# The second cross-attention of a two-layer decoder: the order of its steps, the turning of its maxima, and the order of VectorE's and ScalarE's work

## The chip, the cores and the metric

The kernel runs on one core of one Trainium2 chip. The metric is the device time of one launch in microseconds (us). Before the change it was 882.6 us, the median of three runs (882.2 to 886.55). The profile comes from one further execution, which took 881.06 us.

## The reference, cut to what matters

The reference is a decoder of two layers in float32, on 8 sequences of 128 tokens with 256 features. Each layer has a self-attention, a cross-attention against a context, and a feed-forward part, and after each of them a residual is added and a layer norm taken. The feed-forward part of the second layer is a mixture of 64 experts, of which each token uses 8. The change touches the second layer's cross-attention and the routing that follows:

```
def _L1_xattn_ref(q, k, v):              # x, context, context: (8, 128, 256)
    h = 8                                # the 128 ROWS are split into 8 heads of 16
    qh = q.reshape(b * h, d // h, m)     # (64, 16, 256)
    ...
    qk = jnp.einsum('bdm,bdn->bmn', qh, kh) * scale      # 256 x 256 per head
    sm = jax.nn.softmax(qk, axis=-1)
    ret = jnp.einsum('bmn,bcn->bcm', sm, vh)
    return ret.reshape(b, c, m)
...
x = _layernorm(x + _L1_xattn_ref(x, ctx_2048, ctx_2048), axis=-1)
x = _layernorm(x + _L1_ffn_ref(x, ...), axis=-1)    # logits, softmax, top 8 of 64 experts
```

So the attention runs over the features: in each head 16 rows are contracted and a 256 x 256 matrix of scores is made.

## The kernel before, in words

The program is one straight line of stages. The part in question begins at about 467 us of the profiled execution and ends at about 613 us, when the number of tokens of each expert is known (`full`, L984). After that come the sorting of the token-expert pairs and 104 visits to experts, which need those numbers.

*Heads and units.* The 128 rows of one sequence hold eight heads of 16 rows. They are handled as four blocks of 32 rows (index j, which is also a strip of 32 rows of TensorE), each with two heads, called parity 0 and 1. A unit is a pair (b, par): sequence b, parity par. There are 16 units, worked through by `run_pipelined`: in step n, unit n is in its first stage, unit n-1 in its second, and so on, and within a step the deepest stage is issued first.

*Stages of a unit* (line numbers as in the profile):

- `limits` (L803): GpSimd makes `y_qm`, the rows of this parity alone. TensorE makes scores `y_s` in four tiles, one for each block j (L812), for one half c of the 256 query columns and for both parities, and VectorE takes the negated maximum of each into the tile `maxima` (L820). Half c is tied to par, so both units of a sequence are needed before its maxima are complete.
- `shift` (L824): TensorE turns the maxima of this parity (two transposes, `y_m`, L827). VectorE adds them to `y_qm` (L829) and gives `y_q`. The maxima lie in a row of each head that the other head leaves free; the matching row of `keys` holds ones, so that the next product subtracts the maximum by itself.
- `weights` (L832): eight products `y_sT` (L836), transposed scores less their maximum, then four exponentials `y_e` by ScalarE (L843).
- `weigh` (L848): 16 products with the values (`y_av`) and 16 with ones (`y_z`), both at L855. For parity 1 VectorE then takes the reciprocal of the sums (L862, 128 x 256), multiplies (L864), GpSimd adds the residual (L866), and `layernorm` follows: statistics and their aggregate on VectorE (L187, L189), the reciprocal root on GpSimd (L181, L182), the subtraction and scaling on VectorE (L192).
- `turn_x` (L869), only for five of the units: the normed rows of one or two sequences are written to memory, turned by TensorE (`pt_moe`, L880) and copied by ScalarE (`xT_moe`, L884).
- `choose` (L887): the experts' logits (`gate`, L894), the eight largest (L901), those eight removed (`match_replace`, L903), the mask and the running count `seen`.
- `place` (L912): each pair's position among its expert's (`pos`, L924 and L925; `slot1`, L930), then the softmax over the logits: the exponentials `r_e` on ScalarE (L944), the reciprocal (L949) and the weights `comb` (L951).

The list at L966 gives the depths: limits 0, nothing 1, shift 2, weights 3, weigh 4, nothing 5, turn_x 6, choose 7, place 8. `idle` fills the empty places. In the first three steps `finish_heads` lets TensorE end the self-attention before (`l_y`).

*What sets the order.* `tc.manual_schedule(engines={nc.tensor.engine})` fixes TensorE's order as it is written. The order on VectorE, ScalarE and GpSimd is made by the scheduler of the framework. Each engine works through its own list strictly, and semaphores hold an instruction back until what it needs is there.

*PSUM.* The tiles `y_s`, `y_m`, `y_sT`, `pt_moe`, `gate`, `pos`, `count` and `base` all come from the pool `ps_x` with six banks, handed out in rotation: a tile can be written when the one requested six places earlier has been read by all its readers. `y_av` and `y_z` have two banks of their own.

Of the kernel before, what the change touches and what calls it, by code (L numbers as in the profile page):

```python
# [52 lines left out]


def idle(st, *unit):
    pass
# [3 lines left out]
def decoder_kernel(ctx: ExitStack, tc: tile.TileContext, i, out):  # L60
# [608 lines left out]
    def make_constants():  # L669

        nc.gpsimd.memset(before, 1.0)
        nc.gpsimd.affine_select(
            before, before, pattern=[[1, P]], compare_op=ALU.is_gt, fill=0.0, base=0, channel_multiplier=-1
        )
        nc.gpsimd.iota(iota, pattern=[[1, P]], base=0, channel_multiplier=0, allow_small_or_imprecise_dtypes=True)
        nc.gpsimd.iota(starts, pattern=[[P, P]], base=0, channel_multiplier=0, allow_small_or_imprecise_dtypes=True)
        nc.gpsimd.iota(
            numbers, pattern=[[S, B]], base=0, channel_multiplier=1, allow_small_or_imprecise_dtypes=True
        )
        nc.gpsimd.tensor_scalar(numbers, numbers, 1.0 / (B * S), 1.0, ALU.mult, ALU.add)  # L680
        nc.gpsimd.iota(turns, pattern=[[1, TOP]], base=0, channel_multiplier=0, allow_small_or_imprecise_dtypes=True)
        nc.gpsimd.iota(rows_16, pattern=[[1, P], [0, TOP]], base=0, channel_multiplier=0, allow_small_or_imprecise_dtypes=True)
        nc.gpsimd.tensor_scalar(rows_16, rows_16, -MIDDLE, None, ALU.add)
        nc.gpsimd.iota(blks_16, pattern=[[1, NG], [0, TOP]], base=0, channel_multiplier=0, allow_small_or_imprecise_dtypes=True)
        nc.gpsimd.memset(seen[:, 0, :], 0.0)
        for par in range(2):
            nc.gpsimd.tensor_scalar(keys[:, :, par, :], cx, quarter[par], one_row[par], ALU.mult, ALU.add)
# [87 lines left out]
    with (  # L775
# [4 lines left out]
        tc.manual_schedule(engines={nc.tensor.engine}),  # L780
# [3 lines left out]
        for n in range(2):  # L784
            t = ap.tile([P, 2, 2, P], F32, name=f"maxima_{n}")
            nc.gpsimd.memset(t.rearrange("p a c r -> p (a c r)"), 0.0)
            maxima.append(t)
        for par in range(2):
# [10 lines left out]
            sums_w.append(t.rearrange("p two r -> p (two r)"))  # L799
        def rows_at(j):  # L800
            return slice(32 * j, 32 * j + 32)

        def limits(st, b, par):  # L803
# [12 lines left out]
            flat = maxima[b % 2].rearrange("p par c r -> p (par c r)")  # L816
            for j in range(4):

                at = c * P + 32 * j + 16
                nc.vector.tensor_reduce(  # L820
                    flat[:, at : at + 2 * P - 15 : 2 * P - 16], tiles[j], AX.X, ALU.max, negate=True
                )

        def shift(st, b, par):  # L824
            pt = ps_x(f"y_m_{b}_{par}")[:, : 2 * P]
            for c in range(2):
                nc.tensor.transpose(pt[:, c * P : (c + 1) * P], maxima[b % 2][:, par, c, :], ident)  # L827
            t = xp.tile([P, D], F32, tag=f"qs{par}", name=f"y_q_{b}_{par}")
            nc.vector.tensor_tensor(t, pt, st["q"], ALU.add)  # L829
            st["q"] = t  # L830

        def weights(st, b, par):  # L832
            tiles = [ps_x(f"y_sT_{b}_{par}_{j}").rearrange("p (k m) -> p k m", k=2) for j in range(4)]
            for k in range(2):
                for j in range(4):
                    nc.tensor.matmul(  # L836
                        tiles[j][:, k, :], keys[rows_at(j), b, par, k * P : (k + 1) * P], st["q"][rows_at(j), :],
# [7 lines left out]

        held = {}

        def weigh(st, b, par):  # L848
# [18 lines left out]
            layernorm(x5[b // 2][:, b % 2, :], r, f"l1x_{b}")  # L867

        def turn_x(st, b, par):  # L869

            st["seqs"] = {(1, 1): (0, 2), (3, 1): (2, 2), (5, 1): (4, 2), (7, 0): (6, 1), (7, 1): (7, 1)}.get((b, par))
# [15 lines left out]
        def choose(st, b, par):  # L887
# [12 lines left out]
            for bb in range(n):  # L900
                nc.vector.max(top[:, bb, :], ps[:, bb, :])  # L901

                nc.vector.match_replace(rest[:, bb, :], top[:, bb, :], ps[:, bb, :], -3e38)  # L903
# [6 lines left out]
            st["logits"], st["top"] = ps, top  # L910

        def place(st, b, par):  # L912
# [19 lines left out]
            )  # L932
            if last:
# [3 lines left out]
                )  # L937

            nm = sm.tile([P, 2], F32, tag="nm", name=f"nm_r_{b0}")[:, :n]
            nc.vector.tensor_scalar(nm, st["top"][:, :, 0], -1.0, None, ALU.mult)  # L940
            e = xp.tile([P, 2, NE], F32, tag="r_e", name=f"r_e_{b0}")[:, :n]
            sums = sm.tile([P, 2], F32, tag="sums", name=f"sums_r_{b0}")[:, :n]
            for bb in range(n):
                nc.scalar.activation(  # L944
                    e[:, bb, :], st["logits"][:, bb, :], AF.Exp, bias=nm[:, bb : bb + 1], scale=1.0,
                    accum_out=sums[:, bb : bb + 1],
                )
            inv = sm.tile([P, 2], F32, tag="inv", name=f"inv_r_{b0}")[:, :n]
            nc.vector.reciprocal(inv, sums)  # L949
            for bb in range(n):  # L950
                nc.vector.scalar_tensor_tensor(  # L951
                    comb[:, b0 + bb, :], e[:, bb, :], inv[:, bb : bb + 1], st["mask"][:, bb, :], ALU.mult, ALU.mult
                )
# [3 lines left out]
        def finish_heads(step):  # L957
# [7 lines left out]
        run_pipelined(  # L965
            [(b, par) for b in range(B) for par in range(2)],  # L966
            [limits, idle, shift, weights, weigh, idle, turn_x, choose, place],
            finish_heads,
        )
# [337 lines left out]
```

## Time and profile before

| what | us |
|---|---|
| median of three runs | 882.6 |
| the profiled execution | 881.06 |
| its span, first to last instruction | 879.1 |
| first y_sT starts | 494.21 |
| last y_z ends | 601.96 |
| sequence 7 is normed (L192 ends) | 606.86 |
| `full` ends | 613.2 |
| TensorE busy | 803.5 (91%) |
| VectorE busy | 460.3 (52%) |
| ScalarE busy | 288.7 (33%) |
| mean granted clock of TensorE | 0.954 |

The first two rows are whole times of executions; the span is 1.96 us shorter than the time of its own execution. The other times count from the start of the span. "Busy" counts an engine as working from the recorded start to the recorded end of an instruction; for TensorE the ends are modelled, and waits between the members of a merged group are part of the group's duration. PE is TensorE, PEld its loading of weights, DVE VectorE, ACT ScalarE, POOL GpSimd. In a row of the timeline, the brackets at the end give the idle time of the engine just before, and what ended it. The granted clock is 1.00 at full speed.

### The profile page before, as it was taken

What the parts mean: (1) busy time and instruction counts of PE and PEld (TensorE: products, weight loads), DVE (VectorE), ACT (ScalarE), POOL (GpSimd) and SP (SyncE); (2) the same over time, 40 slices, a digit from 0 to 9 for tenths busy, and PEclk for the clock granted to TensorE, in tenths of its full rate; (3) what the DMA queues carried; (4) which work ended last, traced back from release to release, by engine and by line L of the source; (5) the groups of instructions that cost most, each with busy time, mean ns of one, the idle gap of its engine ahead of it and who ended that gap; (6) DMA issues with size and microseconds to landing.
All of it is one profiled execution on the core that took longest, in us unless ns stands there. A gap on an engine that the chain in (4) does not pass through costs nothing. (4 is left out here: it accounts for less than half of the span.)

```text
span 879.1 us, 14286 instructions
## 1 busy us (share of the span) xinstructions
PE 803.5 (91%) x4588; PEld 539.6 (61%) x4588; DVE 460.3 (52%) x1280; ACT 288.7 (33%) x990; POOL 232.9 (26%) x321
## 2 busy tenths in 40 slices
PE   8899997999999999999999999996588888999945
PEld 5455653667455558555557655553588877988834
DVE  3699886413544442344444566755795333443335
ACT  2567742221333330233330132332232332333301
POOL 0011113215100000000015121101566655555524
PEclk9999987999999999999999998987599999999979
DMA  5500011820000000000000000000579987998665
GB/s 167 157 1 1 2 48 49 293 90 1 0 1 0 1 1 0 1 0 1 1 18 31 1 14 1 13 13 13 198 227 287 296 279 224 299 309 290 203 237 228
DMA packets 39730, 87.80 MB, mean 100 GB/s; under 512 B 6432, under 2 KB 16192, under 8 KB 38752
## 3 DMA queue, kind: packets, MB, share of 16 engines
q1 hardware_dynamic: 32352, 68.96, 24.0%
q0 software_dynamic: 6144, 16.79, 5.7%
q10 hardware_dynamic: 1152, 1.05, 0.4%
q8 instruction: 41, 0.67, 0.3%
q14 instruction: 41, 0.34, 0.1%
HBM read 76.29 MB, written 10.49 MB: 99 GB/s over the span
## 5 line engine op out<-in xcount | busy, mean ns | idle before, releaser
L224 ACT ACTIVATE l_e<-l_s,nm_l 128x128 f32<-128x128 f32 x256 | 90.4, 370 | 93.2 <-DVE nm_l L221 92.9
L1142 PE MATMUL moe_gu_few<-cols,w_few 128*128 (+1 forms) x832 | 114.0, 281 | 2.2 <-issue 0.4
L1142 PEld LDWEIGHTS moe_gu_few<-cols,w_few 128*128 128x128 f32 x832 | 102.9, 195 | 7.5 <-issue 6.6
L1172 POOL DMA_INDIRECT pair_rows<-moe_os_few,pairs x64 | 63.3, 988 | 53.3 <-DVE moe_os_few L1171 41.1
L1096 POOL DMA_INDIRECT xg_few<-x_rows,tok_i x60 | 62.8, 1047 | 29.5 <-issue 11.3
L1159 PE MATMUL moe_o_few<-moe_h_few,w_few 128*128 128x128 f32 x416 | 63.9, 276 | 0.0
L843 ACT ACTIVATE y_e<-y_sT 128x512 f32<-128x512 f32 x64 | 33.0, 603 | 83.3 <-PE y_sT L836 50.6
L740 PE MATMUL l_q<-xT_l1a,w_qkv 128*128 128x512 f32 x128 | 60.2, 593 | 0.0
L740 PE MATMUL l_k<-xT_l1a,w_qkv 128*128 128x512 f32 x128 | 60.1, 592 | 0.0
L740 PE MATMUL l_v<-xT_l1a,w_qkv 128*128 128x512 f32 x128 | 60.1, 592 | 0.0
L231 DVE TENSOR_SCALAR l_e<-l_e,inv_l 128x128 f32<-128x128 f32 x256 | 58.3, 292 | 1.4
L723 DVE TENSOR_TENSOR l_vs<-l_c,l_vs 128x512 f32<-128x512 f32 x32 | 22.1, 692 | 67.4 <-PE l_c L722 67.4
L1162 ACT COPY cols<-moe_o_few 128x256 f32 (+1 forms) x104 | 38.9, 374 | 55.2 <-PE moe_gu_few L1142 18.7
L703 PE MATMUL l_y<-w_o,l_vs 128*128 128x256 f32 x256 | 56.9, 381 | 0.0
L1150 ACT ACTIVATE moe_s_few<-moe_gu_few 128x128 f32<-128x128 f32 x104 | 28.9, 279 | 79.9 <-PE moe_gu_few L1142 39.8
L1159 PEld LDWEIGHTS moe_o_few<-moe_h_few,w_few 128*128 128x128 f32 x416 | 55.2, 193 | 0.0
L703 PEld LDWEIGHTS l_y<-w_o,l_vs 128*128 128x128 f32 x256 | 48.2, 190 | 9.8 <-issue 2.8
L224 ACT ACTIVATION_READ_ACCUMULATOR l_e<-l_s,nm_l 128x1 f32 x256 | 53.2, 208 | 0.0
L1121 DVE COPY cols<-moe_xT_few 128x256 f32<-128x256 f32 x64 | 26.5, 417 | 48.2 <-PE moe_o_few L1159 21.4
L1152 DVE TENSOR_TENSOR moe_h_few<-moe_gu_few,moe_s_few 128x128 f32<-128x128 f32 x104 | 29.7, 286 | 41.5 <-ACT moe_s_few L1150 25.6
L221 DVE TENSOR_REDUCE nm_l<-l_s 128x4 f32<-128x512 f32 x64 | 43.2, 684 | 10.0 <-PE l_s L755 8.1
L748 ACT COPY l_vs<-l_v 128x512 f32<-128x512 f32 x32 | 18.8, 586 | 78.4 <-PE l_v L740 78.4
(267 smaller groups left out, 1360.0 us busy)
## 6 DMA issues: line engine op xcount, KB each, us to landing
w_few<-in_experts SPq DMA_DIRECT2D x104, 384.0 KB
z<-pair_rows SPq DMA_DIRECT2D x7, 1024.0 KB
w_qkv<-in_w_qkv SPq DMA_DIRECT2D x8, 768.0 KB
w_o<-in_w_o SPq DMA_DIRECT2D x1, 2048.0 KB
xT<-in_xT SPq DMA_DIRECT2D x2, 512.0 KB
x<-in_x SPq DMA_DIRECT2D x4, 256.0 KB
cx<-in_ctx SPq DMA_DIRECT2D x1, 1024.0 KB
q_up<-in_up_qT SPq DMA_DIRECT2D x4, 256.0 KB
```

The lines of the kernel that those rows point to most:

```text
L221: nc.vector.tensor_reduce(nm, s, AX.X, ALU.max, negate=True)
L224: nc.scalar.activation(e[:, a, :], s[:, a, :], AF.Exp, bias=nm[:, a : a + 1], scale=1.0, accum_out=sums[:, a : a + 1],)
L231: nc.vector.tensor_scalar(e[:, a, :], e[:, a, :], inv[:, a : a + 1], None, ALU.mult)
L703: nc.tensor.matmul(py[:, :D], scaled[b // 4, m][:, b % 4 * S : (b % 4 + 1) * S], w_o[:, m, :], start=(m == 0), stop=(m == L1_HEADS - 1),)
L740: nc.tensor.matmul(ps, w_qkv[:, k, c, n, :], xT[h][:, k, :], start=(k == 0), stop=(k == 1))
L843: nc.scalar.activation(e, tiles[j], AF.Exp)
L1096: nc.gpsimd.indirect_dma_start(out=x, out_offset=None, in_=xd, in_offset=bass.IndirectOffsetOnAxis(ap=tok_i[:, g : g + 1], axis=0), bounds ...
L1142: mm = nc.tensor.matmul(ps[:, a, :], ws[v][:, at : at + P], cols[:, k, bass.ds(o + P, P)], start=(k == 0), stop=(k == 1),)
L1152: nc.vector.tensor_tensor(hid, ps[:, 1, :], s, ALU.mult)
L1159: nc.tensor.matmul(ps[:, c, :], ws[v][:, at : at + P], hs[v], start=True, stop=True)
L1162: cp = nc.scalar.copy(cols[:, :, bass.ds(o, P)], ps)
L1172: inst = nc.gpsimd.indirect_dma_start(out=zd, out_offset=bass.IndirectOffsetOnAxis(ap=pairs[:, g : g + 1], axis=0), in_=o, in_offset=None, ...
```

## The change

Four things are changed in this part of the kernel.

1. *Order on TensorE.* The stages get explicit depths, and within a step they are issued as weights, weigh, apply, place, choose, turn_x, shift, limits, norm. In steps 18 to 20 it is weights, place, apply, choose, turn_x, weigh, norm, and after that turn_x, choose, place. Sequences 0 to 5 are routed one unit later than before.
2. *Maxima.* The tile `maxima` now holds both parities side by side (16 columns each), so that one pair of transposes turns both. `shift` runs for parity 0 only and makes both `y_q`, each with one scalar_tensor_tensor that keeps one parity's maxima (`one_row[par]`). The order of the two parities in `keys` is swapped to suit.
3. *Order on VectorE and ScalarE.* Both are now under `manual_schedule`: their instructions stand in the order of the program.
4. *Norm and softmax.* `layernorm` is split into `norm` (statistics, root, and a shift made by GpSimd) and `apply` one step later: an activation of ScalarE with scale and bias, except for sequence 7, which VectorE still does. In `choose`, the exponentials of the routing softmax are issued between the eight largest and `match_replace`, and in `place` the weights `comb` come ahead of the count's copy.

```
-        tc.manual_schedule(engines={nc.tensor.engine}),
+        tc.manual_schedule(engines={nc.tensor.engine, nc.vector.engine, nc.scalar.engine}),
...
-            t = ap.tile([P, 2, 2, P], F32, name=f"maxima_{n}")
+            t = ap.tile([P, 2, P], F32, name=f"maxima_{n}")
...
-                at = c * P + 32 * j + 16
-                nc.vector.tensor_reduce(
-                    flat[:, at : at + 2 * P - 15 : 2 * P - 16], tiles[j], AX.X, ALU.max, negate=True
-                )
+                at = c * P + 32 * j
+                nc.vector.tensor_reduce(flat[:, at : at + 17 : 16], tiles[j], AX.X, ALU.max, negate=True)
 
         def shift(st, b, par):
-            pt = ps_x(f"y_m_{b}_{par}")[:, : 2 * P]
+            if par == 1:
+                return
+            pt = ps_x(f"y_m_{b}")[:, : 2 * P]
             for c in range(2):
-                nc.tensor.transpose(pt[:, c * P : (c + 1) * P], maxima[b % 2][:, par, c, :], ident)
-            t = xp.tile([P, D], F32, tag=f"qs{par}", name=f"y_q_{b}_{par}")
-            nc.vector.tensor_tensor(t, pt, st["q"], ALU.add)
-            st["q"] = t
+                nc.tensor.transpose(pt[:, c * P : (c + 1) * P], maxima[b % 2][:, c, :], ident)
+            for par, head in enumerate(states[2 * b : 2 * b + 2]):
+                t = xp.tile([P, D], F32, tag=f"qs{par}", name=f"y_q_{b}_{par}")
+                nc.vector.scalar_tensor_tensor(t, pt, one_row[par], head["q"], ALU.mult, ALU.add)
+                head["q"] = t
...
-            layernorm(x5[b // 2][:, b % 2, :], r, f"l1x_{b}")
+            st["r"] = r
+
+        def norm(st, b, par):
+            if par == 0:
+                return
+            bs = sm.tile([P, 6], F32, tag="ln_st", name=f"st_l1x_{b}")
+            nc.vector.bn_stats(bs, st["r"])
+            mv = sm.tile([P, 2], F32, tag="ln_mv", name=f"mv_l1x_{b}")
+            nc.vector.bn_aggr(mv, bs)
+            rs = sm.tile([P, 1], F32, tag="ln_rs", name=f"rs_l1x_{b}")
+            rsqrt_eps(rs, mv[:, 1:2])
+            if b < B - 1:
+                off = sm.tile([P, 1], F32, tag="ln_shift", name=f"shift_l1x_{b}")
+                nc.gpsimd.tensor_scalar(off, mv[:, 0:1], rs, -1.0, ALU.mult, ALU.mult)
+                mv = off
+            st["mv"], st["rs"] = mv, rs
+
+        def apply(st, b, par):
+            if par == 0:
+                return
+            to = x5[b // 2][:, b % 2, :]
+            if b < B - 1:
+                nc.scalar.activation(to, st["r"], AF.Identity, bias=st["mv"], scale=st["rs"])
+            else:
+                nc.vector.tensor_scalar(to, st["r"], st["mv"][:, 0:1], st["rs"], ALU.subtract, ALU.mult)
...
-            st["seqs"] = {(1, 1): (0, 2), (3, 1): (2, 2), (5, 1): (4, 2), (7, 0): (6, 1), (7, 1): (7, 1)}.get((b, par))
+            st["seqs"] = {(2, 0): (0, 2), (4, 0): (2, 2), (6, 0): (4, 2), (7, 0): (6, 1), (7, 1): (7, 1)}.get((b, par))
...
                 nc.vector.max(top[:, bb, :], ps[:, bb, :])
 
+            nm = sm.tile([P, 2], F32, tag="nm", name=f"nm_r_{b0}")[:, :n]
+            nc.vector.tensor_scalar(nm, top[:, :, 0], -1.0, None, ALU.mult)
...
+            for bb in range(n):
+                nc.scalar.activation(
+                    e[:, bb, :], ps[:, bb, :], AF.Exp, bias=nm[:, bb : bb + 1], scale=1.0,
+                    accum_out=sums[:, bb : bb + 1],
+                )
+            for bb in range(n):
+
                 nc.vector.match_replace(rest[:, bb, :], top[:, bb, :], ps[:, bb, :], -3e38)
...
-        run_pipelined(
-            [(b, par) for b in range(B) for par in range(2)],
-            [limits, idle, shift, weights, weigh, idle, turn_x, choose, place],
-            finish_heads,
-        )
+        units = [(b, par) for b in range(B) for par in range(2)]
+        states = [{} for _ in units]
+        depths = {limits: 0, shift: 2, weights: 3, weigh: 4, norm: 4, apply: 5, turn_x: 6, choose: 7, place: 8}
+        for step in range(len(units) + 8):
+            if step < 18:
+                stages = weights, weigh, apply, place, choose, turn_x, shift, limits, norm
+            elif step < 21:
+                stages = weights, place, apply, choose, turn_x, weigh, norm
+            else:
+                stages = turn_x, choose, place
+            for stage in stages:
+                n = step - depths[stage]
+                if 0 <= n < len(units):
+                    stage(states[n], *units[n])
+            finish_heads(step)
```

## The prediction

> **What bounds the kernel now.** I read the page first: TensorE is busy for 91% of the span, but the share mixes stages. Then the timeline of the second cross-attention. Its matrix work runs from 494 us (first y_sT) to 602 us (last y_z); routing ends at 613.2 us with L984 (full), and everything after it hangs on that instant, so the change is worth what it moves the instant by. TensorE in one step, with the columns start, duration, instruction, idle time before it:
>
> ```profile
> 511.51 2.20 PE L836 MATMUL y_sT<-y_q,keys 32*128 32x256 f32 x16
> 513.65 0.47 PE L827 MATMUL y_m<-ident,maxima 128*128 128x128 f32 x2
> 514.05 2.10 PE L812 MATMUL y_s<-keys,x 32*128 32x512 f32 x8
> 516.08 0.64 PE L855 MATMUL y_av<-y_e,values 128*32 128x256 f32 x8
> ...
> 537.53 1.77 PE L836 MATMUL y_sT<-y_q,keys 32*128 32x256 f32 x16
> 539.23 0.44 PE L827 MATMUL y_m<-ident,maxima 128*128 128x128 f32 x2
> 540.51 3.53 PE L812 MATMUL y_s<-keys,x 32*128 32x512 f32 x8 [0.84 <-ACT r_e L944]
> ```
>
> The same groups take 1.08 (y_sT) and 1.07 us (y_s) where nothing holds them, so 2.20 and 2.10 hide waits inside the groups. The y tiles rotate through six PSUM banks: a tile waits for whoever read the tile six requests earlier. The second to fourth y_s wait for the exponentials of the y_sT just before; the third and fourth y_sT wait for the reductions of the y_s before. VectorE, in the odd steps:
>
> ```profile
> 505.89 1.76 DVE L862 RECIPROCAL y_inv<-y_z 128x256 f32<-128x256 f32 x1 [0.76 <-PE y_z L855]
> 507.68 0.42 DVE L864 TENSOR_TENSOR y_r<-y_av,y_inv 128x256 f32<-128x256 f32 x1
> 508.95 0.43 DVE L187 BATCH_NORM_STATS2 st_l1x<-y_r 128x6 f32<-128x256 f32 x1 [0.84 <-POOL y_r L866]
> 509.41 0.18 DVE L189 BATCH_NORM_AGGREGATE mv_l1x<-st_l1x 128x2 f32<-128x6 f32 x1
> 510.60 0.41 DVE L192 TENSOR_SCALAR x<-y_r,mv_l1x,rs_l1x 128x256 f32<-128x256 f32 x1 [1.01 <-POOL rs_l1x L182]
> ```
>
> VectorE waits twice on GpSimd (0.84 and 1.01) with the reductions queued behind. Last, the stretches view (busy us of PE, PEld, DVE, ACT, POOL, then granted clock):
>
> ```profile
> 505.75:517.94 12.19, 12.19 (x120) 6.39 (x116) 8.84 (x15) 4.13 (x8) 3.39 (x5) 1.00 0.01 1
> 530.73:561.29 30.56, 29.72 (x252) 15.92 (x248) 20.28 (x44) 9.43 (x21) 5.85 (x9) 0.89 0.03 10
> ...
> 538.00:541.40 3.40, 2.56 (x21) 1.47 (x16) 3.16 (x16) 1.64 (x7) 0.00 (x0) 1.00 0.01 2
> 541.40:544.80 3.40, 3.40 (x11) 1.81 (x8) 2.70 (x5) 1.01 (x3) 0.92 (x1) 0.50 0.00 0
> 544.80:548.20 3.40, 3.40 (x34) 1.49 (x33) 0.37 (x2) 0.00 (x0) 0.00 (x0) 0.50 0.00 0
> 568.70:572.10 3.40, 2.56 (x20) 1.53 (x17) 3.13 (x15) 1.78 (x7) 0.00 (x0) 1.00 0.00 0
> ```
>
> Two plain steps take 12.19 us; four steps with a routing group take 30.56. Inside each routing group the clock falls to 0.50 for 6.8 us, both times after 3.4 us in which TensorE was busy for only 2.56. In 541.4 to 548.2 the y_av/y_z group took 3.4 us, not 1.84, and y_s 3.53, not 2.53: one fall costs about 2.6 us.
>
> **The change, part by part.** In each step TensorE now runs y_sT, y_av/y_z, (routing), y_m, y_s instead of y_av/y_z, y_sT, y_m, y_s. The weighting now lies between y_sT and y_s, where it hides the exponentials, and no longer between y_s and the next y_sT, where it hid the reductions. VectorE, in program order: reciprocal and multiply (odd steps), routing, y_q, four reductions, statistics.
>
> *Odd step, laid out from the end of the weighting.* Reciprocal 1.76 and multiply 0.42 stand ahead of the reductions: 2.2. The y_s (1.07) are done by then. The fourth y_sT needs the second reduction, 0.60 + 0.68 later: 3.5. Weight load after the wait and its two halves: about 0.95, so the weighting starts at 4.45 and ends at 6.3 (1.84).
> *Even step.* One pair of turns 0.37, y_s 1.07 + 0.1 to VectorE, 1.28 for two reductions, 0.95, then 1.84: 5.75. The two y_q are now SCALAR_TENSOR_TENSOR from PSUM: between 0.42 (L829) and 0.48 (L1231), taken at 0.47 as L569, which also reads PSUM (0.463). They run during the y_s, so either bound costs nothing; without that cover it would be 0.1 a pair. Pair: 12.05 against 12.19. Gains on one side (half of the 32 turns, 8 x 0.37 = 3.0; the two waits for GpSimd; the exponentials) are spent on the exposed reductions.
>
> *Routing group, full clock.* turn_x adds four turns, 0.6. choose stands ahead of the reductions, and in the changed program match_replace waits for ScalarE's two exponentials (both read the gate bank): two MAX8 0.45, nm 0.16, exponentials 2 x (0.31 + 0.19) = 1.0, replaces 0.6, mask 0.23, seen 0.45, together 2.9. place (0.75 pos on TensorE, then slot 0.28, inv 0.15, two combine 0.5 ahead of y_q) delays the reductions by about 1.05. Sum 4.55 over four plain steps, so 28.65 where before took 30.56 and 29.46, each with a fall.
>
> *First and last steps.* The weighting of the first head pair starts 4.6 after the first y_sT (1.08 + 1.17 + 1.28 + 0.95, nothing to weigh yet), at 498.8, against 498.18. From there to the weighting of (7, 0): 7 pairs x 12.05 = 84.35, two routing groups 9.1, less 5.4 because the last two intervals have no y_s: 586.9. Before: about 593.0, so 6.1 earlier, of which 5.2 are the two falls.
>
> *Tail.* On ScalarE the last apply by activation (sequence 6) stands ahead of the copy of xT_moe for sequences 4 and 5. It needs reciprocal, multiply, add, statistics and GpSimd's root and shift (1.76 + 0.42 + 0.73 + 0.61 + 0.22 + 0.57 + 0.22, with the hops 5.0), counted from 1.7 before the weighting of (7, 0): 3.3. Then 0.60 for the activation (L1243, the same form; 0.37 as a copy is the lower bound) and 0.59 for the copy: 4.5. Queued behind that copy on TensorE are gate and the last weighting, which before ran without a break: gate to 5.6, weighting to 7.45. VectorE's choose for 4 and 5 (2.9) delays the last reciprocal to 8.5. Then 3.2 for VectorE, 1.0 for GpSimd, 0.41: sequence 7 is normed 13.15 after 586.9, at 600.05 (before 606.87). From there before took 6.33. Now gate 6 follows the turns of 7, choose 6 stands ahead of choose 7, and each has its exponential in the line to the mask: about 1.8 more. End 608.2 against 613.2: minus 5.0, if the clock never falls between 494 and 600.
>
> *The clock.* In an odd step TensorE works about 1.8 of the 3.4 us after the weighting (y_s, two y_sT, then waiting), less than the 2.56 that twice preceded a fall. A 3.4 us slice that begins within about 1.8 us there is this empty: chance about one half in each of the four plain odd steps with reductions, so 2. In the two choose steps the wait is 2.9 longer: 0.9 each. Together about 4 falls at 2.6: plus 10.4. Bounds: 0 (nothing falls) and 6 (every odd step), plus 15.6.
>
> [...] The slice at 538.0 was three quarters busy and the clock fell all the same, so the sum goes by the row.
>
> Sum against the profiled execution: 881.06 (span 879.1) - 5.0 + 10.4 = 886.5. The median, 882.6, is 1.5 above it: 888.0. Change: +5.4, where 0.5% (4.4 us) is about what can be told from no change.
>
> **The rivals.**
> *The clock holds (other side).* Place: the odd steps. With at most one fall the time is 877.6 to 880.2; it decides below two falls (5.0 / 2.6). For it: the work per pair is the same as before, and plain steps show clock 1.00 now. Against: before spread its waits over each step, this gathers them after the weighting.
> *As many falls as now.* Two, in the choose steps alone: 882.6 - 5.0 + 5.2 = 882.8.
> *VectorE streams.* If the layout is too strict and TensorE never waits on a reduction, a pair costs VectorE's own sum: 8 x 0.62 + 2.2 + 0.95 + 0.61, and gaps, about 9. Seven pairs save 20: some 868. Against: the third y_sT waits by bank, whatever VectorE's total.
> *More falls, longer tail.* Six: 893.2, and the tail's half clock may begin earlier, another 2.
> *The edit moves nothing.* A pair comes out equal anyway; this falls in with the second rival.
>
> **How the numbers follow.** Three to five falls: 0.54, centre 888.0 (885.4 to 890.6). Two falls: 0.15. None or one: 0.15. VectorE streams: 0.05. Six or more: 0.11. The range leaves out 0.05 of streaming and a little at both ends: 877 to 896. Faster by over 0.5% (below 878.2): streaming 0.05 and most of the no-fall cases, 0.13 together. Within: the rest of those, two falls, and most of three: 0.32. Slower (above 887.0): 0.55.
>
> **What would show it.** Pairs of plain steps near 12 us; in odd steps y_sT groups of 3 us or more with TensorE waiting for maxima; match_replace after r_e; a gap of about 2.5 us on TensorE ahead of gate for 4 and 5; VectorE no longer waiting 1.0 for rs_l1x but once; four stretches of clock 0.5 between 494 and 600. Wrong if that count is below two, if reductions run during the reciprocal's step without delay, or if the tail takes no longer than now.

## The result and the profile after

The changed kernel takes 889.12 us (median of 14 runs, 884.51 to 894.63), the kernel before, on the same chip, 882.42 (14 runs, 878.15 to 886.55). The medians differ by 6.7 us (0.8%); the ratio on record is 1.010, with a 95% interval of 1.0078 to 1.0123. So it is slower, by about 1%.

The profiled execution of the changed kernel took 890.04 us. Its head, its sums and two rows of 40 equal slices, from the page (sums: engine, busy us, share, instructions; the rows: PE is TensorE's busy share in tenths, PEclk its granted clock in tenths):

```profile
span 888.3 us, 14266 instructions
PE 797.9 (90%) x4572; PEld 537.9 (61%) x4572; DVE 458.2 (52%) x1273; ACT 293.1 (33%) x997; POOL 233.4 (26%) x328
PE   8899988999999999999999998986598888998855
PEclk9999996999999999999999979887599999999979
```

The same two rows of the kernel before:

```profile
PE   8899997999999999999999999996588888999945
PEclk9999987999999999999999998987599999999979
```

TensorE is busy for less (797.9 us against 803.5), and the kernel is slower all the same. The slices from the 23rd to the 28th, in which the part in question lies, show why sums over the span say little here: TensorE is less busy there (9, 9, 8, 9, 8, 6 against 9, 9, 9, 9, 9, 6), and its clock is lower on the whole (9, 7, 9, 8, 8, 7 against 9, 9, 8, 9, 8, 7).

From here on "the stage" is the stretch from the start of the first y_sT to the end of `full`. It took 118.99 us before and takes 126.83 now, 7.84 more. The rest of the 9 us between the two profiled executions lies behind `full` (265.9 against 267.4 us), where nothing was changed.

A plain odd step on TensorE now (timeline; start, duration, instruction, idle time before it and what ended it):

```profile
520.17 0.64 PE L853 MATMUL y_av<-y_e,values 128*32 128x256 f32 x8
...
522.04 1.14 PE L810 MATMUL y_s<-keys,x 32*128 32x512 f32 x8
523.00 0.60 PE L836 MATMUL y_sT<-y_q,keys 32*128 32x256 f32 x4
525.04 1.73 PE L836 MATMUL y_sT<-y_q,keys 32*128 32x256 f32 x12 [1.45 <-DVE maxima L818]
526.70 0.82 PE L853 MATMUL y_av<-y_e,values 128*32 128x256 f32 x8
```

VectorE in the same step:

```profile
522.17 1.76 DVE L860 RECIPROCAL y_inv<-y_z 128x256 f32<-128x256 f32 x1 [1.92 <-PE y_z L853]
523.96 0.42 DVE L862 TENSOR_TENSOR y_r<-y_av,y_inv 128x256 f32<-128x256 f32 x1
524.31 2.48 DVE L818 TENSOR_REDUCE maxima<-y_s 128x2 f32<-128x512 f32 x4
526.70 0.42 DVE L871 BATCH_NORM_STATS2 st_l1x<-y_r 128x6 f32<-128x256 f32 x1
```

Before, the waits hid inside the groups (y_s 2.10, y_sT 2.20). Now y_s is short (1.14), but the wait inside y_sT has grown and come out into the open: its first four instructions run through in 0.60, the other twelve start after 1.45 of idle time, and from start to end it lasts 3.77 (523.00 to 526.77). VectorE is idle for 1.92 until the sums `y_z` are there, then the reciprocal and the multiplication hold the reductions back to 524.31, and the third y_sT waits for them.

The stretches view (length, then busy us and instructions of PE, PEld, DVE, ACT, POOL, then granted clock). The whole stage comes first, in the kernel before and then in the changed one; after that come, all from the changed kernel, the 3.4 us ahead of three of the falls, and then one slice that no fall follows:

```profile
494.21:613.20 118.99, 110.97 (x977) 60.97 (x976) 75.60 (x176) 38.01 (x85) 20.61 (x34) 0.91 0.03 10
...
494.10:620.90 126.80, 106.42 (x961) 58.80 (x960) 73.51 (x168) 42.13 (x92) 21.71 (x41) 0.85 0.03 9
...
506.54:509.95 3.41, 1.96 (x17) 0.95 (x14) 3.09 (x4) 0.10 (x1) 0.72 (x1) 1.00 0.03 5
523.61:527.02 3.41, 1.98 (x20) 1.21 (x24) 3.38 (x7) 0.57 (x2) 0.72 (x1) 1.00 0.03 5
...
550.92:554.33 3.41, 2.12 (x16) 1.18 (x15) 2.64 (x5) 0.59 (x4) 0.72 (x1) 1.00 0.00 0
...
567.98:571.39 3.41, 2.07 (x24) 0.79 (x16) 2.73 (x4) 0.46 (x1) 0.40 (x1) 1.00 0.00 0
```

The mean clock of the stage is 0.85 (0.91 before). The clock falls to 0.50 at 510.0 (for 6.8 us), 527.0 (3.4), 540.7 (3.4), 554.3 (6.8) and 585.0 (6.8), always in or at the end of an odd step, then for 3.4 at 605.5 in the tail, and from 612.4 on. Before there were two falls, at 541.4 and 572.1, each of 6.8, and the tail's from 606.3.

### The profile page after: what moved, and what is told of

Same layout as the page of the kernel before. It is cut to its first block, busy times and chain, and to the rows that moved or that the text cites. A ratio compares the mean times of both kernels' runs of the same rounds, so it can differ in the third digit from the quotient of the medians.

```text
span 888.3 us, 14266 instructions
## 1 busy us (share of the span) xinstructions
PE 797.9 (90%) x4572; PEld 537.9 (61%) x4572; DVE 458.2 (52%) x1273; ACT 293.1 (33%) x997; POOL 233.4 (26%) x328
## 5 line engine op out<-in xcount | busy, mean ns | idle before, releaser
L1177 PE MATMUL moe_gu_few<-cols,w_few 128*128 (+1 forms) x832 | 115.9, 284 | 2.0 <-issue 1.0
L1177 PEld LDWEIGHTS moe_gu_few<-cols,w_few 128*128 128x128 f32 x832 | 104.7, 197 | 6.5 <-issue 5.7
L1197 ACT COPY cols<-moe_o_few 128x256 f32 (+1 forms) x104 | 38.8, 373 | 50.9 <-PE moe_o_few L1194 21.3
L836 PE MATMUL y_sT<-y_q,keys 32*128 32x256 f32 x256 | 40.1, 449 | 12.2 <-DVE maxima L818 6.4
```

The costliest lines, as they stand in the source:

```text
L836: nc.tensor.matmul(tiles[j][:, k, :], keys[rows_at(j), b, 1 - par, k * P : (k + 1) * P], st["q"][rows_at(j), :], start=True, stop=True,)
L1177: mm = nc.tensor.matmul(ps[:, a, :], ws[v][:, at : at + P], cols[:, k, bass.ds(o + P, P)], start=(k == 0), stop=(k == 1),)
L1197: cp = nc.scalar.copy(cols[:, :, bass.ds(o, P)], ps)
```

## The experiments

The chips differ: for e1 to e4 and e9 to e11 what lies behind the stage, the visits to experts above all, takes some 240 us, for e5 to e8 some 265, as in the runs above. So a time is compared only with that of the kernel before on the same chip; the expectations of the first four runs gave their times for a chip of the slower kind, and there the ratio and the stage decide. The ratio is the one on record; that of the two medians can differ from it by two or three thousandths. The stage is from each profiled execution. The kernel before was profiled only on the first chip, so its stage of 118.99 stands for all chips.

| run | us | before, same chip | ratio (95%) | stage |
|---|---|---|---|---|
| e1_after_filled | 855.09 | 853.28 | 1.0025 (1.001 to 1.0039) | 118.9 |
| e2_before_filled | 848.32 | 853.28 | 0.9931 (0.9905 to 0.9957) | 112.6 |
| e3_weigh_first | 839.16 | 853.28 | 0.9821 (0.9794 to 0.9847) | 102.2 |
| e4_scheduler | 850.44 | 853.28 | 0.9958 (0.9941 to 0.9974) | 113.8 |
| e5_changed_again | 887.2 | 878.76 | 1.0109 (1.0047 to 1.017) | 126.9 |
| e6_copy_first | 885.05 | 878.76 | 1.0064 (1.0028 to 1.0099) | 123.3 |
| e7_replace_first | 884.32 | 878.76 | 1.0057 (1.0027 to 1.0086) | 122.5 |
| e8_mended | 861.16 | 878.76 | 0.9806 (0.9754 to 0.9858) | 98.9 |
| e9_weigh_first_scheduler | 846.29 | 853.35 | 0.9905 (0.9874 to 0.9935) | 107.4 |
| e10_joint_maxima | 851.64 | 853.35 | 0.9983 (0.9961 to 1.0004) | 116.0 |
| e11_norm_by_scalar | 866.98 | 853.35 | 1.0167 (1.0081 to 1.0252) | 127.8 |

The second table is worked out from the timelines: the time from the start of one weighting (first y_av of a unit) to the next. An odd step follows the weighting of a unit of parity 1, so VectorE's reciprocal is in it; an even step follows one of parity 0. A plain step is one without routing and, in e4, without half clock. "Choose" is the step with the choice of experts for two sequences, "place" the next one, with their positions. A star marks a value with half clock in it.

| run | plain odd | plain even | choose | place |
|---|---|---|---|---|
| before | 5.77 | 6.43 | 9.46* | 7.27* |
| after | 6.52 to 7.47* | 7.43* to 7.88* | 10.41* | 7.63* |
| e1_after_filled | 6.53 | 5.79 | 9.46 | 6.59 |
| e3_weigh_first | 5.28 | 5.77 | 5.77 | 6.63 |
| e4_scheduler | 6.34 | 6.10 | 7.42 | 6.28 |
| e10_joint_maxima | 5.27 | 6.59 | 9.6* | 6.82* |

In before and e10_joint_maxima the routing stands one unit earlier, so there choose falls in an even step and place in an odd one; in the other rows it is the other way round.

### The falls of the clock: e1_after_filled and e2_before_filled

In the changed kernel products that give nothing to the result are put ahead of y_sT in the odd steps, where TensorE waits:

```
         def weights(st, b, par):
             tiles = [...]
+            if par == 1 and (b, par) != (7, 1):
+                for _ in range(18 if b in (4, 6) else 6):
+                    nc.tensor.matmul(tiles[0][:, 0, :P], ident, ones, start=True, stop=True)
```

> The changed kernel, with TensorE kept busy where it waits for the reductions: ahead of the y_sT of every second head of a pair it writes 6 products of 128x128 (18 in the two steps behind a choose) into the first y_sT tile, which the true product overwrites. Results are unchanged. Theory (each fall of the clock after such a wait costs about 2.6 us): no or one stretch of half clock between 494 and 600 us instead of five, time 889.1 - 4 or 5 x 2.6 + about 1 for the fillers = 877 to 880. Rival (VectorE's reductions set the pace, and the clock falls only while TensorE has nothing to do): the clock is full and the time stays at 887 to 891.

In the kernel before, six such products are put ahead of the turns in two steps, those of its two falls:

```
         def shift(st, b, par):
             pt = ps_x(f"y_m_{b}_{par}")[:, : 2 * P]
+            if (b, par) in ((4, 0), (6, 0)):
+                for _ in range(6):
+                    nc.tensor.matmul(pt[:, :P], ident, ones, start=True, stop=True)
```

> The kernel before, with 6 such products ahead of the turns of the maxima (y_m) of the two units whose step holds the fall of the clock. Theory: the two stretches of half clock at 541 and 572 us go, time 882.4 - 2 x 2.6 = 877. Rival: the clock holds and the time stays at 882.

A filled odd step of the changed kernel (timeline of TensorE):

```profile
505.93 1.14 PE L810 MATMUL y_s<-keys,x 32*128 32x512 f32 x8
507.00 1.60 PE L836 MATMUL y_sT<-ones,ident 128*128 128x128 f32 x12
508.54 2.13 PE L839 MATMUL y_sT<-y_q,keys 32*128 32x256 f32 x16
510.60 0.64 PE L856 MATMUL y_av<-y_e,values 128*32 128x256 f32 x8
```

The weighting follows y_s's start by 4.67 (510.60 - 505.93), as without the filling (526.70 - 522.04 = 4.66), so the filling costs the step nothing, and none of the five falls is left: the clock first falls at 593.3. In the choose step the 18 products cost nothing either: from the start of the reductions to the weighting it is 2.39 there (548.61 to 551.00), as in the plain odd step of the changed kernel (524.31 to 526.70). The stage goes from 126.8 to 118.9, the ratio from 1.010 to 1.0025. That is some 7 us, less than the 9 to 12 that the theory gave. The kernel before gains from the same filling too: both its falls are gone (only the tail's, from 603.8, stays), its stage shrinks by 6.4 and its time by 5.0. So the falls come from TensorE having too little to do in these slices, and the fall is a price of its own, beside the wait.

What the five falls cost can be read from the second table's sources, since e1_after_filled is the same program at full clock there: summed from the first weighting to that of unit (7, 0), the intervals are 100.69 us in the changed kernel and 90.46 filled. That is 10.2, or 2.05 for each fall; the stage shrinks by 2.3 less because the filled run's first weighting came 1.2 later and its tail was 1.1 longer.

### The order of the steps and the order on VectorE and ScalarE: e3, e4 and e9

The weighting goes ahead of y_sT again, everything else is as changed:

```
-                stages = weights, weigh, apply, place, choose, turn_x, shift, limits, norm
+                stages = weigh, weights, apply, place, choose, turn_x, shift, limits, norm
```

> The changed kernel with one thing undone: within a step the weighting stands ahead of the y_sT again, all else as in the change. Theory (the loss is the reductions, uncovered by turning the steps round): the y_sT no longer wait 1.45 us for the maxima, a pair of plain steps takes about 11 us in place of 12 to 14, at most two or three falls of the clock in the steps, end of the routing some 20 us earlier: 866 to 872, below the kernel before. Rival (the loss comes from VectorE's program order, its reciprocal, choose and the wait for ScalarE ahead of the reductions): these stay, time 883 or more.

The steps stay turned round, but the order on VectorE and ScalarE is the scheduler's again:

```
-        tc.manual_schedule(engines={nc.tensor.engine, nc.vector.engine, nc.scalar.engine}),
+        tc.manual_schedule(engines={nc.tensor.engine}),
```

> The changed kernel with VectorE and ScalarE ordered by the scheduler again; TensorE's turned order, the joint turning of the maxima and the norm by ScalarE stay. Theory (the turned steps are the main loss): the odd steps still wait for the maxima, three or more falls, 881 to 886, and the gap on TensorE ahead of the gate of sequences 4 and 5 is smaller. Rival (program order on VectorE and ScalarE is the loss): 878 or less, below the kernel before.

And both edits at once:

> Both undone: weighting first, and VectorE and ScalarE ordered by the scheduler; the joint turning of the maxima and the norm by ScalarE stay. It completes the square of the two orders (stage from the first y_sT to full: turned and program order 126.8, turned and scheduler 113.8, weighting first and program order 102.2). Theory (the two work together: program order costs only where the steps are turned, and is a small gain otherwise): 104 to 107. Rival (program order by itself makes the stage quick once the weighting is first): 112 or more.

An odd step of e3_weigh_first on TensorE, then on VectorE (timelines):

```profile
505.49 0.64 PE L853 MATMUL y_av<-y_e,values 128*32 128x256 f32 x8
...
506.81 0.61 PE L853 MATMUL y_z<-y_e,sums_w 128*32 128x256 f32 x8
507.35 1.15 PE L836 MATMUL y_sT<-y_q,keys 32*128 32x256 f32 x16
508.32 2.52 PE L810 MATMUL y_s<-keys,x 32*128 32x512 f32 x8
510.76 0.64 PE L853 MATMUL y_av<-y_e,values 128*32 128x256 f32 x8
```

```profile
507.49 1.76 DVE L860 RECIPROCAL y_inv<-y_z 128x256 f32<-128x256 f32 x1 [0.75 <-PE y_z L853]
509.28 0.42 DVE L862 TENSOR_TENSOR y_r<-y_av,y_inv 128x256 f32<-128x256 f32 x1
509.62 2.48 DVE L818 TENSOR_REDUCE maxima<-y_s 128x2 f32<-128x512 f32 x4
```

VectorE does the same work in the same order as in the changed kernel, but nothing on TensorE waits for it: y_sT runs through in 1.15, and the reductions, late as they are (509.62), lie beside the next weighting. What TensorE waits for is inside y_s (2.52 for 1.07 of work), where it waits for the exponentials; the loads of weights for y_s wait 8.2 us in 29 waits for the exponentials between 494 and 600 us, and that costs less than what it replaces. A pair takes 11.05 (5.28 + 5.77) instead of 12.32 at full clock, a choose step 5.77 instead of 9.46, and no fall comes before 589.9. The kernel is 14.1 us faster than before: the turned order of the steps alone costs 24.6 us of stage. Of these 10.2 are the five falls, 10.0 the steps at full clock (90.46 against 80.44 from the first weighting to that of unit (7, 0)), 1.5 the start and 2.9 the tail.

With the scheduler's order the turned steps look like this (e4_scheduler, VectorE):

```profile
509.08 1.76 DVE L860 RECIPROCAL y_inv<-y_z 128x256 f32<-128x256 f32 x1 [1.92 <-PE y_z L853]
510.76 0.63 DVE L818 TENSOR_REDUCE maxima<-y_s 128x2 f32<-128x512 f32 x1
511.30 0.41 DVE L862 TENSOR_TENSOR y_r<-y_av,y_inv 128x256 f32<-128x256 f32 x1
511.62 1.88 DVE L818 TENSOR_REDUCE maxima<-y_s 128x2 f32<-128x512 f32 x3
```

The scheduler puts one reduction ahead of the multiplication, and in the choose steps three of the four reductions ahead of match_replace (7.42 instead of 9.46 at full clock). Two short falls are left of five. The time is 0.9958 of before; the theory gave at best a tie and at least three falls, the rival 878 or less on the slower kind of chip, which is 0.995, so the theory was missed and the written order underrated.

| stage, us | VectorE and ScalarE as written | by the scheduler |
|---|---|---|
| y_sT ahead of the weighting (changed) | 126.8 | 113.8 (e4) |
| the weighting ahead of y_sT | 102.2 (e3) | 107.4 (e9) |

So the two parts can't be judged one by one: the written order costs 13.0 where the steps are turned, and gains 5.1 where they are not (107.38 against 102.24; the theory of e9 had 104 to 107). There the plain pairs are equal (11.04 and 11.05); the difference lies in the two place steps (7.72 and 5.66 by the scheduler, 6.63 and 4.57 as written) and in the last interval (5.90 and 3.38, with a short fall at its end in e9), and 0.4 lie behind that.

### The tail and match_replace: e5, e6, e7

The changed kernel once more, as the measure for e6 to e8, which ran on the same chip:

> The changed kernel as it is, beside the kernel before on the chip of these runs, where the visits to experts go quicker (853 us in all for the kernel before). Theory (the loss lies between the first y_sT and the end of the routing): 6 to 9 us more than the kernel before here too, and that stage again about 127 us against 119. Rival (part of the loss lies in the visits, which begin later): less than 4 or more than 11 us.

It agrees with the first measurement (1.0109 against 1.010, the same seven stretches of half clock to 0.1 us, the two of the tail among them, stage 126.9). For the tail, `apply` goes behind `turn_x` in steps 18 to 20, so that ScalarE copies xT_moe first:

```
-                stages = weights, place, apply, choose, turn_x, weigh, norm
+                stages = weights, place, choose, turn_x, apply, weigh, norm
```

> The changed kernel with one swap in steps 18 to 20: apply stands behind turn_x, so that ScalarE copies xT_moe of sequences 4 and 5 before its activation for sequence 6. Theory (the gap of 2.47 us on TensorE ahead of the gate of 4 and 5 is on the path): the gap falls below 0.5, the end of the routing comes 2.0 to 2.5 earlier. Rival (VectorE's reciprocal for sequence 7 would be late anyway, behind choose): less than 0.7 earlier.

ScalarE and TensorE in the changed kernel's tail, and TensorE in that of e6_copy_first (timelines):

```profile
603.03 0.60 ACT L887 ACTIVATE x<-y_r,shift_l1x,rs_l1x 128x256 f32<-128x256 f32 x1 [1.98 <-POOL shift_l1x L878]
603.54 0.56 ACT L906 COPY xT_moe<-pt_moe 128x512 f32<-128x512 f32 x1
```

```profile
601.06 0.61 PE L853 MATMUL y_z<-y_e,sums_w 128*32 128x256 f32 x8
604.15 1.10 PE L916 MATMUL gate<-gate,xT_moe 128*128 128x64 f32 x8 [2.47 <-ACT xT_moe L906]
605.19 0.80 PE L853 MATMUL y_av<-y_e,values 128*32 128x256 f32 x8
```

```profile
602.33 0.61 PE L853 MATMUL y_z<-y_e,sums_w 128*32 128x256 f32 x8
602.88 1.10 PE L916 MATMUL gate<-gate,xT_moe 128*128 128x64 f32 x8
603.91 0.64 PE L853 MATMUL y_av<-y_e,values 128*32 128x256 f32 x8
```

The copy, whose data TensorE had turned by 599.5, stood behind an activation that waited for GpSimd; with the copy first, the 2.47 are gone. The stage is 3.5 shorter, more than the 2.0 to 2.5 expected: the tail from (7, 0) to `full` takes 18.05 instead of 21.21, since the short fall at 605.5, behind the gap, is gone too, and the last fall ahead of the tail came later and was shorter (590.0, 3.4 us). The time is 2.2 below that of e5_changed_again, though the intervals of the two overlap.

In e7_replace_first `match_replace` is issued ahead of the exponentials, as in the kernel before:

```
             for bb in range(n):
                 nc.vector.max(top[:, bb, :], ps[:, bb, :])
+            for bb in range(n):
+                nc.vector.match_replace(rest[:, bb, :], top[:, bb, :], ps[:, bb, :], -3e38)
...
-            for bb in range(n):
-                nc.vector.match_replace(rest[:, bb, :], top[:, bb, :], ps[:, bb, :], -3e38)
```

> The changed kernel with match_replace ahead of nm and the exponentials again, as in the kernel before. Theory (the wait for ScalarE's exponentials, 0.77 in the log of VectorE, stands in the line to the reductions and twice in the last routing): about 1.0 less in each of the two choose steps, 1.0 ahead of the last reciprocal, 0.5 to 1 in the last routing, together 3.5 to 4.5 less, more if a fall of the clock goes too. Rival (the choose steps wait for something else as soon as this wait is gone): less than 1.5.

VectorE in a choose step, first in the changed kernel, then in e7_replace_first:

```profile
583.59 0.35 DVE L923 MAX8 r_top<-gate 128x8 f32<-128x64 f32 x2
583.97 0.53 DVE L926 TENSOR_SCALAR nm_r<-r_top 128x2 f32<-128x2 f32 x1
585.26 0.09 DVE L936 MATCH_VALUE_LOAD r_rest<-r_top,gate 128x8 f32 x1 [0.77 <-ACT r_e L930]
...
586.45 2.48 DVE L818 TENSOR_REDUCE maxima<-y_s 128x2 f32<-128x512 f32 x4
```

```profile
553.46 0.35 DVE L923 MAX8 r_top<-gate 128x8 f32<-128x64 f32 x2
553.73 0.08 DVE L925 MATCH_VALUE_LOAD r_rest<-r_top,gate 128x8 f32 x1
...
554.94 2.48 DVE L818 TENSOR_REDUCE maxima<-y_s 128x2 f32<-128x512 f32 x4
```

From the first MAX8 to the reductions it is 2.86 in the changed kernel and 1.48 here. With two such steps and the tail the stage shrinks by 4.4, the time by 2.9 against e5_changed_again, where the intervals overlap again. The falls stay (five before 600, at other places).

### The parts alone, in the kernel before: e10 and e11

Only the maxima of both parities side by side, turned at once, and the two scalar_tensor_tensor:

```
-            t = ap.tile([P, 2, 2, P], F32, name=f"maxima_{n}")
+            t = ap.tile([P, 2, P], F32, name=f"maxima_{n}")
...
         def shift(st, b, par):
-            pt = ps_x(f"y_m_{b}_{par}")[:, : 2 * P]
+            if par == 1:
+                return
+            pt = ps_x(f"y_m_{b}")[:, : 2 * P]
...
```

> The kernel before with one part of the change: both heads' maxima side by side, turned at once in the first head's shift, two scalar_tensor_tensor for y_q. Theory (the turns of the second head, 8 x 0.37, and their waits are on TensorE's path): the stage 2.5 to 3.5 shorter than 119.0, the time 2.5 to 3.5 less than the kernel before. Rival (TensorE waits for the exponentials at that place anyway): within 1 of the kernel before.

The stage is 3.0 shorter, near the 8 x 0.37 of the turns saved: odd steps take 5.27 instead of 5.77, but even steps 6.59 instead of 6.43, so a pair gains 0.34; the first weighting comes 0.5 earlier. The two falls stay where they were. In the time it is 1.7 us, less than the 2.5 to 3.5 expected, with an interval that reaches 1.0004: in the stage the gain is there, in the time it can't be told from nothing with certainty.

Only the norm's last step by ScalarE, in the order of the scheduler, for all sequences but the last:

```
-            layernorm(x5[b // 2][:, b % 2, :], r, f"l1x_{b}")
+            ...                       # bn_stats, bn_aggr, rsqrt_eps as in layernorm
+            nc.gpsimd.tensor_scalar(off, mv[:, 0:1], rs, -1.0, ALU.mult, ALU.mult)
+            nc.scalar.activation(to, r, AF.Identity, bias=off, scale=rs)
```

> The kernel before with one part of the change: the norm's last step by ScalarE, shift by GpSimd, in the stage where it stood, except for sequence 7. Theory (the scheduler puts the activation on ScalarE ahead of the next exponentials, which then wait for GpSimd's root, 1.2 with the shift): every second step some 2 longer, the stage 4 to 10 longer than 119.0. Rival (VectorE's seven waits of 1.0 for rs_l1x go and nothing else changes): 3 to 6 shorter.

ScalarE in this run (timeline), and TensorE behind it:

```profile
505.90 1.58 ACT L843 ACTIVATE y_e<-y_sT 128x512 f32<-128x512 f32 x3 [3.70 <-PE y_sT L836]
509.88 0.60 ACT L879 ACTIVATE x<-y_r,shift_l1x,rs_l1x 128x256 f32<-128x256 f32 x1 [2.40 <-POOL shift_l1x L878]
510.39 0.57 ACT L843 ACTIVATE y_e<-y_sT 128x512 f32<-128x512 f32 x1
```

```profile
511.01 0.40 PE L855 MATMUL y_av<-y_e,values 128*32 128x256 f32 x1 [1.80 <-ACT y_e L843]
```

The scheduler put the activation between the third and the fourth exponential; it waits 2.40 for GpSimd's shift, the fourth exponential behind it, and the weighting waits 1.80 for that. The stage is 8.8 longer, with four short falls ahead of 600 us; the time is 13.6 longer, from four runs that lie between 858.39 and 871.17, and what the other 4.8 are stays open. In the changed kernel `apply` stands one step later, and its four waits for the shift come to 2.5 in all, 1.98 of them in the tail. So what the activation on ScalarE costs hangs on its place. What it gains by itself, in the place that the program gives it, no run shows.

### The parts put right: e8_mended

The three edits of e3, e6 and e7 in the changed kernel:

> The changed kernel with three things mended: weighting ahead of y_sT in the steps up to 17, apply behind turn_x in steps 18 to 20, match_replace ahead of the exponentials. Theory (the three add up): the run with the weighting first took 14.1 less than the kernel before on its chip; 3 to 5 more go, so 17 to 19 less than the kernel before, and the stage lasts 97 to 99 us. Rival (with the weighting first the two small ones are covered): 13 to 15 less.

The time is 861.16 against 878.76 for the kernel before, 17.6 less, a ratio of 0.9806 (0.9754 to 0.9858), the stage 98.94 against 118.99, with no fall before 591.3: the three add up, as the theory had it. It beats both kernels. A plain pair takes 11.04, a choose step 5.76.

In these runs the time gains less than the stage does: 14.1 against 16.8 in e3, 17.6 against 20.1 in e8, 5.0 against 6.4 in e2. Why is not shown; the stage of the kernel before, which was profiled on another chip, is one of the two numbers.

## Why the prediction was right

The sum gave +5.4 in the profiled execution's stage; +7.84 was measured there, and +6.7 in the medians. The direction holds, and so does the main reason: the waits gathered behind the weighting bring more falls of the clock. But the falls are little more than half of the loss. Taking the steps at full clock from the two filled runs, the difference of 7.84 falls into four parts:

| part | laid out | measured |
|---|---|---|
| first y_sT to first weighting | +0.6 | +0.96 |
| steps to the weighting of (7, 0), at full clock | -1.5 | +1.68 (90.46 against 88.78) |
| falls | +5.2 (10.4 - 5.2) | +4.16 (10.23 - 6.07) |
| tail to `full` | +1.1 | +1.04 |
| sum | +5.4 | +7.84 |

So the shorter chains, which were to save 1.5, save nothing: even at full clock the turned steps are slower. That 5.4 lies so near the 6.7 of the medians is in part luck.

*Step by step, from the first y_sT, against the changed kernel.* The first weighting was laid out 4.6 after it and came after 4.93. From there to the weighting of (7, 0), the sum at full clock was 88.1 (586.9 - 498.8); filled, the same program took 90.46: 2.4 too little, the term of the sum that was mis-sized. Of it 1.9 are the pairs, 12.32 instead of 12.05 (odd 6.53 for 6.3, even 5.79 for 5.75), seven times. The rest is the balance of two errors: the two routing groups took 0.8 less than the 9.1 laid out (about 4.2 each for 4.55), and the last two intervals, without y_s, saved 4.2 instead of 5.4. The 5.75 for the even step lies nearer to the measured 5.79 than the terms given for it, which add up to 5.61 (0.37, 1.17, 1.28, 0.95 and 1.84). In the odd step the 0.95 from the second reduction to the weighting was 1.11 (525.59 to 526.70). The falls were 10.4 and cost 10.2. The tail from (7, 0) to `full` was 21.3 (608.2 - 586.9) and took 21.21, by two errors that cancel: sequence 7 was normed 0.5 later than laid out, with half clock in the last weighting, and the rest took 0.6 less. Together 0.3 + 2.4 - 0.2 - 0.1 = 2.4, which is the difference of 7.84 to 5.4.

*The falls.* Their sum is right by luck, by two errors that cancel: five instead of four, at 2.05 instead of 2.6 each. The 2.6 came from one fall of before; e2_before_filled shows that a long fall there cost 3.0 ((9.46 - 7.99) + (7.27 - 5.77)), and in the changed kernel the long ones cost 3.0, 2.0 and 1.9, the two short ones 1.6. The places were as laid out: three of the four plain odd steps (one half was taken for each) and both choose steps (0.9 each).

*Busy time and the falls.* TensorE was busy for 1.96, 1.98 and 2.12 of 3.41 us ahead of three falls and never idle for a whole slice, and the clock fell to 0.50. But busy time alone does not decide: the slice at 567.98, with 2.07, brought none. The traces agree better with another count, which weighs each product by its recorded form. Take for each product its columns (512 for a row with 32x512) times its share of 128*128, the largest form recorded (a quarter for y_s, y_sT, y_av and y_z, recorded as 32*128 or 128*32; all of it for those of 128*128, as the turns and the gate), spread evenly over its recorded time. Then the slices ahead of the five falls hold 1446, 1004, 866, 1471 and 1516 columns, those ahead of the two falls before 1292 and 1304, and the slice at 567.98 holds 1862. In all thirteen profiles the steps, from the first y_sT to the last weighting, hold 301 such slices at full clock, laid out in steps of 3.41 us from each run's first fall: of the 36 with the least work (1516 or less) 34 were followed by a fall, of the other 265 none. By busy time they do not part: a slice with 3.12 us busy was followed by a fall, and 40 with less were not. This count was made from the traces afterwards; no run was made to test it, and the two slices out of line (879 and 1458, both in e11_norm_by_scalar) are not explained.

*choose.* 2.9 were laid out and 2.86 measured, with match_replace waiting for ScalarE's exponentials as written. The gap ahead of the gate for 4 and 5 was to be about 2.5 and is 2.47, and e6_copy_first shows its cause.

*The rivals.* "The clock holds" did not come about, and e1_after_filled tells what it would have been worth: not 5.0 faster, but a stage of 118.9, as before, since the layout was 2.4 too short and that run's own start and tail took 2.3 more. The rival of two falls, in the choose steps alone, is out as well: three more came in plain odd steps. "VectorE streams" fails where it was said to, at the third y_sT. Nothing in the prediction saw that the order of two stages, under VectorE's written order, held the loss, and not the maxima or the norm: the prediction compared the two ends and found a pair equal (12.05 against 12.19), and never priced the pair with the weighting first and the rest as changed, which takes 11.05.

## What to carry to other kernels

Where an engine's queue is written out in program order, ask first which of its long instructions (here a reciprocal of 1.76) stands ahead of work that TensorE needs in the same step: here the written order lost 13.0 us where the reductions were due in the same step, and gained 5.1 where they had a weighting's time more. When a change has several parts, cost each with the others held, in both orders: here the rest of the change was worth 16.8 us of stage (118.99 against 102.2), and the turned order of the steps took 24.6 again. Of the 16.8, e10_joint_maxima shows 3.0 for the joint turning and e2_before_filled some 6 for the two falls that e3 does not have; how the rest divides no run shows. And look at what TensorE's products come to in a slice, weighed by their form, not only at whether it is busy: here the turned steps cost 10.0 us at full clock, and the falls of the clock that came with their gathered waits another 10.2.

## What the runs showed that was not expected

Products whose result is thrown away made both kernels faster: six in each of two steps took 5.0 us off the kernel before, and those in the odd steps took the changed one's ratio from 1.010 to 1.0025. Within the steps the half clock comes in stretches of 3.4 or 6.8 us (in the tail of some 31 or 34 as well), and repeats at the same places from run to run (e5_changed_again and the first profile agree to 0.1 us). The chips differ by 3% in time (853 against 879 and 882 us for the same kernel), and the difference lies behind the stage, in the part with the visits to experts, some 240 against 265 us. Plain pairs of steps are equal (11.05 in e3, 11.04 in e8).
